# Spreading per-token scales over all partitions through DRAM instead of TensorE transposes, in an audio tower on one core

## The chip, the cores and the metric

The kernel runs on one core of a Trainium2 chip. A core has five engines with queues of their own: TensorE (PE in the profile; PEld is its loading of stationary operands), VectorE (DVE), ScalarE (ACT), GpSimd (POOL) and SyncE (SP), which issues most DMAs. They wait for one another by semaphores only. SBUF is the working memory of 128 partitions, PSUM holds what TensorE writes, and DRAM lies outside of the core. The metric is the device time of one execution in microseconds (us), a median over runs.

## What is computed

The input is 64 clips of 80000 samples. Each clip is padded and cut into 157 frames of 512 samples, which are the tokens, of width 512. One layer follows:

```
h = frames @ DCT.T                        # tokenizer, float32
n = (h - mean) / sqrt(var + 1e-5)         # layer norm over the 512 features of a token
V, g = n @ Wv + bv, sigmoid(n @ Wg + bg)
kp, qp = tanh(n @ Wk + bk) * pi, tanh(n @ Wq + bq) * pi
total = causal sums over tokens of V, weighted by cos(key phase - query phase), and by position
total = g * total + (1 - g) * positional part, divided by sqrt(8 * position)
h = h + n + total @ Wo + bo
m = layer norm of h
e = argmax of softmax(mean over tokens of m @ Wg2 + bg2)   # one of 16 experts per clip
h = h + score[e] * (m @ We[e] + be[e])
```

All of it is in float32.

## The kernel before

**Tiling.** The clips go in 16 groups of `GB` = 4. The tokens of a clip are padded to 160, five blocks of 32; a tile of 128 partitions holds one block of each of the four clips, so a group has five tiles: 0 to 3 and `TAIL` (4). The samples of a group lie in `xT` with the features on the partitions and the 640 tokens in the free dimension, in two halves of 320 (`half`).

**Where the scale comes in.** The layer norm needs 1 / deviation of every token (`rstd`). The DCT is linear and its weights are already less their mean, so the kernel projects the *samples* with the DCT folded into `wv`, `wg` and `wkq`, and multiplies the samples by 1 / deviation first. A token's deviation is found from the tokens laid on partitions (`embed`, then `statistics`: two VectorE instructions and three small ones on GpSimd, with a fourth in `embed_statistics`), so it is a column, one value per partition. The samples need it as a row, the same in all 128 partitions. `scale_all` does that turn: six TensorE transposes of a broadcast column against the identity (L298) leave the rows in PSUM, and two VectorE multiplications (L304) scale the halves of `xT`.

**Stages of a group g from the second on.** `project_and_values(g)`: phases and value products from `xT` (with `turn_x2(g-1, n)` between them, which turns the normalized block n of the group before by four transposes, L690, for its expert). `gate(g)`. `experts_and_embedding(g)`: the expert products of group g-1 (L817), one block at a time, and between them the embedding and statistics of group g+1. `attention(g)`: `read` (L614) sums the values over tokens, then come the output products. Group 0 has its own opening (`first_values`, `first_gate`).

**The output products.** `attention` multiplies by `Wo` in the Strassen-Winograd manner: seven products (`output_product`, L372) in the order 1, 2, 6, 7, 4, 5, 3. Products 3, 6 and 7 take sums of tokens that `token_sums` makes on VectorE, one or two at a `next(made)`: sums 0 and 1 (product 6), 2 (product 7), 3 (product 3). The last tile has its own product (`output_tail`, L237) after product 1. VectorE adds each product from PSUM to the residual, whose quarters are `r11`, `r12` (blocks 0 and 1) and `r21`, `r22` (blocks 2 and 3). After product 7, three additions go to GpSimd (`more`, L630; on VectorE in the last group); products 4 and 5 are added to `r21` and `r22` behind them. After product 5 `statistics2` takes blocks 2 and 3, and `normal2` normalizes a block on ScalarE (L677). `scale_all(g+1)` stands after product 7.

**What sets the order.** The order of the program is that of the Python code (`manual_schedule`): every engine takes its instructions in that order, and the framework puts in the semaphore waits between engines. Buffers rotate: `psum()` gives one of four PSUM tiles in turn, and a TensorE product waits until the tile's last reader is done. Tiles of one tag share buffers in the same way; `even` has two.

Of the kernel before, what the change touches and what calls it, by code (L numbers as in the profile page):

```python
# [14 lines left out]
F32 = mybir.dt.float32  # L15
I32 = mybir.dt.int32
AF = mybir.ActivationFunctionType
ALU = mybir.AluOpType
# [4 lines left out]
P = 128  # L23
C = D // P
H = D // 2
GB = 4
NG = B // GB
LP = 160
Q = P // GB
NM = LP // Q  # L30
TAIL = NM - 1
SLOT = [0, 1, 3, 4, 2]
HT = P // 2
HN = HT + 2 * P
# [19 lines left out]
def audio_tower(ctx: ExitStack, tc: tile.TileContext, a, out):  # L54
# [21 lines left out]
    nc = tc.nc  # L76
    ctx.enter_context(tc.manual_schedule())
    pool = lambda name, bufs, **kw: ctx.enter_context(tc.tile_pool(name=name, bufs=bufs, **kw))
    const = pool("const", 1)
    p1 = pool("p1", 1)  # L80
    p2 = pool("p2", 2)
    small = pool("small", 8)
    ps_mm = pool("ps_mm", 4, space=bass.MemoryType.PSUM)

    def load(name, shape, src=None):
        t = const.tile(shape, F32, name=name, tag=name)
# [3 lines left out]
    def psum():  # L90

        return ps_mm.tile([P, 2, 512], F32, tag="mm", name="mm")
# [4 lines left out]
    S = [{} for _ in range(NG)]  # L97
# [120 lines left out]
        sub(raw, raw, ps.unsqueeze(1).to_broadcast([P, C, n]))  # L218


    def statistics(h):

        st = small.tile([P, 6], F32, tag="st", name="st")
        nc.vector.bn_stats(st, h)
        mv = small.tile([P, 2], F32, tag="mv", name="mv")
        nc.vector.bn_aggr(mv, st)  # L226
        rstd = small.tile([P, 1], F32, tag="rstd", name="rstd")
        nc.gpsimd.tensor_scalar(rstd, mv[:, 1:2], EPS, None, ALU.add)  # L228
        nc.gpsimd.tensor_tensor(rstd, rstd, power, ALU.pow)  # L229
        shift = small.tile([P, 1], F32, tag="shift", name="shift")  # L230
        nc.gpsimd.tensor_scalar(shift, mv[:, 0:1], rstd, -1.0, ALU.mult, ALU.mult)  # L231
        return rstd, shift

    def by_tokens(ps, x, n, w):

        for c in range(C):
            nc.tensor.matmul(ps, tile_of(x[:, c], n), w[:, c, :], start=(c == 0), stop=(c == C - 1))  # L237
        return ps


    def embed(g, n):
# [15 lines left out]
    def embed_statistics(g, n):  # L257
        s = S[g]
        h, odd = s.pop(("h", n))
        by_r = h.rearrange("p (j r) -> p r j", r=4)  # L260
        sines = p2.tile([P, P + 1], F32, tag="sines", name="sines")
        nc.scalar.copy(sines, odd[:, 1, : P + 1])
        add(by_r[:, 1, :], odd[:, 0, :P], sines[:, :P])
        sub(by_r[:, 3, :], odd[:, 0, 1 : P + 1], sines[:, 1 : P + 1])
        rstd, shift = statistics(h)
        rstd1 = small.tile([P, 1], F32, tag="rstd1", name="rstd1")
        nc.gpsimd.tensor_scalar(rstd1, rstd, 1.0, None, ALU.add)  # L267
        s["rstd", n] = rstd
        s["st", n] = h, shift, rstd1

    def embed_res(g, n):

        s = S[g]
        h, shift, rstd1 = s.pop(("st", n))
        if n == TAIL:
            r = p1.tile([P, D], F32, tag="res_t", name="res_t", bufs=2)
        else:
            if n % 2 == 0:
                s["res2"].append(p1.tile([P, 2, D], F32, tag="res", name="res", bufs=6))
            r = s["res2"][-1][:, n % 2, :]  # L280
        nc.scalar.activation(r, h, AF.Identity, bias=shift, scale=rstd1)  # L281
        s["res"][n] = r

    def add_bo(g, n):
        r = S[g]["res"][n]
        nc.gpsimd.tensor_tensor(r, r, bo, ALU.add)  # L286

    def scale_all(g):

        s = S[g]  # L290
        ps = psum()
        lo = 0

        for n in (0, 1, TAIL, TAIL, 2, 3):
            rows = slice(0, P) if n != TAIL else slice(0, HT) if lo < HN - 1 else slice(HT, P)
            m, at = divmod(lo, HN)
            w = rows.stop - rows.start
            nc.tensor.transpose(  # L298
                ps[:, m, at : at + w], s["rstd", n][rows].to_broadcast([w, P]), ident[rows, rows]
            )  # L300
            lo += w
        for m in range(2):
            x = half(s["xT"], m)
            nc.vector.tensor_tensor(x, x, ps[:, m, :HN].unsqueeze(1).to_broadcast([P, C, HN]), ALU.mult)  # L304


    def quarters(w):
# [316 lines left out]
    def output_product(g, i):  # L624

        s = S[g]
        ps = product(g, i, fac_o)
        (r11, r12), (r21, r22) = ([r[:, :, n : n + H] for n in (0, H)] for r in s["res2"])
        last = g + 1 == NG
        more = lambda to, x: (nc.vector if last else nc.gpsimd).tensor_tensor(to, to, x, ALU.add)  # L630
        if i == 1:
            s["u"] = [p2.tile([P, 2, H], F32, tag="u", name="u") for _ in range(2)]
            nc.scalar.copy(s["u"][0], ps)  # L633
        first, second = s["u"]
        if i in (1, 2):
            add(r11, ps, r11)
            if last and i == 2:
                add_bias(g - 1, ORDER[0])
        elif i == 6:
            add(first, ps, first)  # L640
        elif i == 7:
            add(second, ps, first)
            more(r22, second)
            more(r21, second)
            more(r12, first)
        elif i == 5:
            add(r22, ps, r22)
            if last:
                add(r12, ps, r12)
            for n in (2, 3):  # L650
                statistics2(g, n)
            if not last:
                add(r12, ps, r12)
        elif i == 3:
            add(r12, ps, r12)
        else:
            add(r21, ps, r21)
# [150 lines left out]
    def add_bias(g, n):  # L808

        s = S[g]  # L810
        nc.vector.scalar_tensor_tensor(s["res"][n], s["be"], s["gate"], s["res"][n], ALU.mult, ALU.add)
# [25 lines left out]
    def expert(g, n, between=lambda c: None):  # L837
        ps = psum()
        for c in range(C):
            between(c)  # L840
            expert_chunk(g, n, c, ps[:, 0, :])
        between(C)
        expert_out(g, n, ps[:, 0, :])
# [82 lines left out]
    def first_gate():  # L926

        made = chain(weight_sums(wv, t_v), weight_sums(wo, t_o))

        def weights():  # L930
            next(made)
            next(made)

        gate_part(0, 0)
        weigh()
        fold_twice(1, 1)
        add_bo(0, 0)
        gate_part(0, 1)
        weights()
        scores(0)  # L940
        embed(1, 2)
        embed_statistics(1, 2)
        embed_res(1, 2)
        add_bo(0, 1)
        weights()
        weights()
        gate_part(0, 2)
        for n in (3, TAIL):
            embed(1, n)
            embed_statistics(1, n)  # L950
        for n in (3, TAIL):
            embed_res(1, n)
        weights()
        gate_part(0, 3)
        for n in (2, 3, TAIL):
            add_bo(0, n)
        load_half(2, 0)
        load_half(2, 1)
# [62 lines left out]
    def experts_and_embedding(g):  # L1021

        new = g + 1

        def embedded(n):
            embed_statistics(new, n)
            embed_res(new, n)

        add_bias(g - 1, TAIL)
        expert(g - 1, TAIL)  # L1030
        for n in range(3):
            embed(new, n)
            embed_statistics(new, n)
        add_bias(g - 1, 0)
        for n in range(3):
            embed_res(new, n)
        add_bv(g, 0)
        load_half(g + 2, 0)
        load_half(g + 2, 1)
        expert(g - 1, 0)  # L1040
        add_bias(g - 1, 1)
        add_bv(g, 1)
        expert(g - 1, 1)
        embed(new, 3)
        embed(new, TAIL)
        embed_statistics(new, 3)
        embed_statistics(new, TAIL)
        embed_res(new, 3)
        embed_res(new, TAIL)
        add_bias(g - 1, 2)  # L1050
        expert(g - 1, 2)
        add_bias(g - 1, 3)
        expert(g - 1, 3)

    def attention(g):
        ahead = g + 1 < NG
        if ahead and g > 0:
            for n in range(NM):
                add_bo(g + 1, n)
        for c in range(C):  # L1060
            read(g, c)
        S[g]["blocks"] = halves(S[g]["gT"])
        made = token_sums(g, tail=False)
        if g == 0:
            for n in range(NM):
                add_bo(1, n)
        for i in (1, 2, 6, 7, 4, 5, 3):
            output_product(g, i)
            if i == 1:
                next(made)  # L1070
                next(made)
                output_tail(g)
                statistics2(g, TAIL)
            elif i in (2, 6):
                next(made)
                if i == 6:
                    normal2(g, TAIL)
            elif i == 7 and ahead:
                scale_all(g + 1)
        for n in (0, 1):  # L1080
            statistics2(g, n)
        normal2(g, 2)
        normal2(g, 3)
# [170 lines left out]
```

## Time and profile before

The median is 1384.3 us over three runs (1384.22 to 1384.72); the profiled execution spans 1382.9 us, with the TensorE clock granted in full.

| what | from the profile |
|---|---|
| TensorE, VectorE, ScalarE, GpSimd busy | 99%, 75%, 29%, 44% of the span |
| transposes of the scale, L298 | 96, in 16 groups |
| multiplications of the samples, L304 | 32, 1.48 us each (median) |
| additions on GpSimd, L630 | 45, 1.27 us each |
| DMA from DRAM of half a group's samples, 640 KB | 4.5 us from issue to landing |
| DMA of an output block, 64 KB | 1.7 us |

A row of the groups reads: line, engine, operation, out<-in by the program's names, shapes, count, and after the bar the busy time in us, the mean ns of one, and the idle time of the engine just before with what ended it. A row of the timeline reads: start and duration in us, engine, line, operation, names, shapes, count, and in brackets the idle time before it and its releaser. Rows of one kind that follow each other are merged. Starts on TensorE are pipelined: the next matmul starts before the row's end, so the cost of a matmul in the queue is the distance between starts, not its duration.

### The profile page before, as it was taken

How to read it: one execution, taken by the hardware profiler on the slowest of the kernel's cores; microseconds unless marked ns; L12 is line 12 of the kernel's file. 1: busy time of each engine (PE TensorE's matmuls, PEld its weight loads, DVE VectorE, ACT ScalarE, POOL GpSimd, SP SyncE). 2: the span in 40 equal slices, each digit the busy share in tenths (PEclk: the TensorE clock that was granted, in tenths of full speed). 3: DMA queues.
4: the chain of work that ended last, by engine and by line, in shares of the span. 5: the costliest groups of instructions: out<-in, count | busy, mean ns of one | idle time of the engine just before them, and what ended most of it. 6: DMA issues, size and time to landing. Idle time of an engine off the chain costs nothing.

```text
span 1382.9 us, 26934 instructions
## 1 busy us (share of the span) xinstructions
PE 1374.0 (99%) x10656; PEld 918.0 (66%) x10656; DVE 1031.8 (75%) x2076; ACT 403.3 (29%) x690; POOL 607.2 (44%) x858
## 2 busy tenths in 40 slices
PE   9999999999999999999999999999999999999998
PEld 5676575866758567575765758667585675757763
DVE  5888786877868677786777868778686777867673
ACT  2514142231423214242141422314232142421410
POOL 2462554425453354544525544254533535445314
PEclk9999999999999999999999999999999999999999
DMA  6013214032230413205032140322304132040306
GB/s 224 1 39 130 76 55 145 9 135 72 108 99 1 169 38 130 77 3 188 16 130 77 52 146 9 136 72 115 91 1 157 50 130 77 4 150 16 130 9 197
DMA packets 47292, 119.70 MB, mean 87 GB/s; under 512 B 9264, under 2 KB 26304, under 8 KB 39232
## 3 DMA queue, kind: packets, MB, share of 16 engines
q0 software_dynamic: 11456, 72.10, 13.6%
q1 hardware_dynamic: 35212, 45.26, 11.1%
q8 instruction: 84, 1.38, 0.4%
q10 hardware_dynamic: 500, 0.64, 0.2%
q14 instruction: 40, 0.33, 0.1%
HBM read 97.39 MB, written 20.58 MB: 85 GB/s over the span
## 4 chain that ended last, share of the span: by engine, by line
PE 99%; DVE 0%; DMA 0%; issue 0%; SPq 0%
PE mm L372 27%; PE mm L817 21%; PE mm L579 17%; PE mm L614 9%; PE mm L237 9%; PE mm L252 3%; PE mm L690 3%; PE mm L524 3%; PE mm L254 3%; PE mm L560 1%; PE mm L598 1%; PE mm L298 1%; PE mm L198 1%; DMA wv<-in_wv 0%; PE mm L709 0%; PE mm L736 0%
## 5 line engine op out<-in xcount | busy, mean ns | idle before, releaser
L817 PE MATMUL mm<-we,x2T 128*32 128x512 f32 x2400 | 268.1, 594 | 0.4 <-issue 0.4
L228 POOL TENSOR_SCALAR rstd<-mv 128x1 f32<-128x1 f32 x160 | 42.8, 267 | 508.0 <-DVE mv L226 498.0
L817 PEld LDWEIGHTS mm<-we,x2T 128*32 128x32 f32 x2400 | 73.3, 110 | 162.6 <-issue 158.4
L99 DVE TENSOR_TENSOR gT<-mm,gT 128x128 f32<-128x128 f32 (+1 forms) x135 | 87.0, 673 | 82.3 <-PE mm L579 80.9
L622 DVE TENSOR_TENSOR gT<-mm,gT 128x320 f32<-128x320 f32 x256 | 116.9, 488 | 26.1 <-PE mm L614 21.7
L614 PE MATMUL mm<-att,v 32*128 32x256 f32 (+3 forms) x2048 | 124.1, 360 | 0.0
L614 PEld LDWEIGHTS mm<-att,v 32*128 32x128 f32 x2048 | 105.2, 185 | 22.8 <-ACT res_t L281 6.7
L589 ACT ACTIVATE gT<-gT,hbg 128x320 f32<-128x320 f32 x120 | 59.7, 556 | 168.2 <-DVE gT L99 168.2
L229 POOL TENSOR_TENSOR rstd<-rstd,power 128x1 f32<-128x1 f32 x160 | 98.3, 614 | 13.3
L828 DVE SCALAR_TENSOR_TENSOR res<-mm,gate,res 128x512 f32<-128x512 f32 x64 | 48.0, 750 | 73.1 <-PE mm L817 63.8
L677 ACT ACTIVATE x<-res,shift,rstd 128x512 f32<-128x512 f32 x64 | 52.1, 816 | 142.7 <-DVE res L99 126.1
L771 POOL DMA_INDIRECT we<-in_we,rows x60 | 62.2, 1036 | 71.3 <-DVE rows L767 57.6
L372 PE MATMUL mm<-t_o,sum 128*128 128x256 f32 x384 | 88.3, 379 | 0.4 <-DVE sum L98 0.4
L121 POOL TENSOR_TENSOR xT<-xT 128x640 f32<-128x640 f32 x30 | 46.8, 1559 | 91.6 <-DVE even L99 84.7
L99 DVE TENSOR_TENSOR v<-mm,v 128x512 f32<-128x512 f32 x105 | 70.8, 686 | 18.8 <-PE mm L372 18.4
L372 PE MATMUL mm<-t_v,sum 128*128 128x256 f32 x360 | 82.7, 379 | 0.0
L286 POOL TENSOR_TENSOR res<-res,bo 128x512 f32<-128x512 f32 x64 | 82.2, 1314 | 0.0
L231 POOL TENSOR_SCALAR shift<-mv,rstd 128x1 f32<-128x1 f32 x160 | 73.8, 461 | 16.6
L281 ACT ACTIVATE res<-mm,shift,rstd 128x512 f32<-128x512 f32 x64 | 49.8, 778 | 104.2 <-POOL rstd L267 79.7
L372 PEld LDWEIGHTS mm<-t_o,sum 128*128 128x128 f32 x384 | 71.9, 190 | 11.7 <-PE mm L372 0.8
L99 DVE TENSOR_TENSOR res<-mm,res 128x512 f32<-128x512 f32 x96 | 65.2, 685 | 15.0 <-ACT u L633 11.8
L630 POOL TENSOR_TENSOR res<-res,u 128x512 f32<-128x512 f32 x45 | 56.0, 1273 | 42.1 <-DVE u L99 42.1
(199 smaller groups left out, 2799.2 us busy)
## 6 DMA issues: line engine op xcount, KB each, us to landing
xT<-in_frames SPq DMA_DIRECT2D x32, 640.0 KB, 4.5
out<-res SPq DMA_DIRECT2D x236, 64.0 KB, 1.7
out<-res_t SPq DMA_DIRECT2D x62, 32.0 KB, 1.6
out<-res_t SPq DMA_DIRECT2D x62, 26.0 KB
wv<-in_wv SPq DMA_DIRECT2D x2, 512.0 KB, 6.0
wg<-in_wg SPq DMA_DIRECT2D x1, 1024.0 KB
wo<-in_wo SPq DMA_DIRECT2D x1, 1024.0 KB
we<-in_we,rows POOLq DMA_INDIRECT x60
```

Source lines behind the costliest of these rows:

```text
L99: add = lambda *x: nc.vector.tensor_tensor(*x, ALU.add)
L229: nc.gpsimd.tensor_tensor(rstd, rstd, power, ALU.pow)
L231: nc.gpsimd.tensor_scalar(shift, mv[:, 0:1], rstd, -1.0, ALU.mult, ALU.mult)
L237: nc.tensor.matmul(ps, tile_of(x[:, c], n), w[:, c, :], start=(c == 0), stop=(c == C - 1))
L286: nc.gpsimd.tensor_tensor(r, r, bo, ALU.add)
L372: nc.tensor.matmul(ps[:, b, :], lhs[:, c, P * b : P * (b + 1)], w[:, c, :], start=(c == 0), stop=(c == 1))
L579: nc.tensor.matmul(ps[:, o, :HN], w[:, c, o * P : (o + 1) * P], rhs[:, c], start=(c == 0), stop=(c == 1))
L589: nc.scalar.activation(to, to, AF.Tanh, bias=hbg[:, c : c + 1], scale=0.5)
L614: nc.tensor.matmul(to, s["v", n][q, c * P : (c + 1) * P], by, start=(n == 3), stop=(n == TAIL))
L622: nc.vector.tensor_tensor(th, r[:, :, n], th, op)
L771: nc.gpsimd.indirect_dma_start(out=ws[b][:, n * k : n * (k + 1)], out_offset=None, in_=of, in_offset=bass.IndirectOffsetOnAxis(ap=rows[:, ...
L817: nc.tensor.matmul(ps[Q * i : Q * (i + 1), :], s["x2T"][:, c, i, Q * n : Q * (n + 1)], s["ws"][i][:, c, :], start=(c == 0), stop=(c == C - 1),
```

## The change

From group 1 on the turn of the scale goes another way. `statistics` writes 1 / deviation of the new group straight into a column of a 128x32 tile (`deviations`, two of them in turn, set to zero at the start). `keep_deviations` transposes this tile on VectorE, in blocks of 32x32, so that each clip's values become rows of 32, and four small DMAs write them to DRAM in the order of the samples' tokens. `spread_deviations` reads that row of 640 values back into all partitions with one DMA, into an `even` buffer. The purpose is that TensorE has no transposes for it. `scale_all` then multiplies the samples by this SBUF tile. It is called after product 1, ahead of the last tile's product, with all three of the first token sums ahead of it; the fourth sum is made after product 7. In product 7 the addition to `r21` goes ahead of that to `r22`. Group 0 keeps its transposes.

```diff
+    dram = pool("dram", 2, space=bass.MemoryType.DRAM)
...
-    def statistics(h):
+    def statistics(h, rstd=None):
...
-        rstd = small.tile([P, 1], F32, tag="rstd", name="rstd")
+        if rstd is None:
+            rstd = small.tile([P, 1], F32, tag="rstd", name="rstd")
...
+    deviations = [const.tile([P, Q], F32, name=f"dev{k}", tag=f"dev{k}") for k in range(2)]
+    for x in deviations:
+        nc.gpsimd.memset(x, 0.0)
...
-        rstd, shift = statistics(h)
+        if g == 0:
+            to = None
+        else:
+            to = deviations[g % 2][:, SLOT[n] : SLOT[n] + 1]
+        rstd, shift = statistics(h, to)
...
+    def keep_deviations(g):
+
+        turned = p2.tile([P, Q], F32, tag="turned", name="turned")
+        nc.vector.transpose(turned, deviations[g % 2])
+        S[g]["row"] = row = dram.tile([NM, GB, Q], F32, tag="row", name="row")
+        for i in range(GB):
+            nc.sync.dma_start(out=row[:, i], in_=turned[Q * i : Q * i + NM])
+
+    def spread_deviations(g):
+
+        s = S[g]
+        s["scale"] = scale = p2.tile([P, 2, HN], F32, tag="even", name="scale")
+        row = s.pop("row").rearrange("s b t -> (s b t)")
+        nc.sync.dma_start(out=scale.rearrange("p m t -> p (m t)"), in_=row.partition_broadcast(P))
...
         for m in range(2):
             x = half(s["xT"], m)
-            nc.vector.tensor_tensor(x, x, ps[:, m, :HN].unsqueeze(1).to_broadcast([P, C, HN]), ALU.mult)
+            nc.vector.tensor_tensor(x, x, scale[:, m, :HN].unsqueeze(1).to_broadcast([P, C, HN]), ALU.mult)
...
             add(second, ps, first)
+            more(r21, second)
             more(r22, second)
-            more(r21, second)
             more(r12, first)
...
+        keep_deviations(1)
+        spread_deviations(1)
         weights()
         gate_part(0, 3)
...
         expert(g - 1, 2)
+        keep_deviations(new)
         add_bias(g - 1, 3)
         expert(g - 1, 3)
+        spread_deviations(new)
...
             if i == 1:
-                next(made)
-                next(made)
+                for _ in range(3):
+                    next(made)
+                if ahead:
+                    scale_all(g + 1)
                 output_tail(g)
                 statistics2(g, TAIL)
-            elif i in (2, 6):
+            elif i == 6:
+                normal2(g, TAIL)
+            elif i == 7:
                 next(made)
-                if i == 6:
-                    normal2(g, TAIL)
-            elif i == 7 and ahead:
-                scale_all(g + 1)
```

More of the change, by code (lines that the diff above doesn't have):

```diff
@@ L286, in add_bo @@
         nc.gpsimd.tensor_tensor(r, r, bo, ALU.add)
+    def keep_deviations(g):
[9 more added lines that the diff above has]
+        nc.sync.dma_start(out=scale.rearrange("p m t -> p (m t)"), in_=row.partition_broadcast(P))
     def scale_all(g):
         s = S[g]
[L291 to L301, printed above, removed]
+        if g == 0:
+            scale = psum()
+            lo = 0
+            for n in (0, 1, TAIL, TAIL, 2, 3):
+                rows = slice(0, P) if n != TAIL else slice(0, HT) if lo < HN - 1 else slice(HT, P)
+                m, at = divmod(lo, HN)
+                w = rows.stop - rows.start
+                nc.tensor.transpose(
+                    scale[:, m, at : at + w], s["rstd", n][rows].to_broadcast([w, P]), ident[rows, rows]
+                )
+                lo += w
+        else:
+            scale = s.pop("scale")
         for m in range(2):
             x = half(s["xT"], m)
-            nc.vector.tensor_tensor(x, x, ps[:, m, :HN].unsqueeze(1).to_broadcast([P, C, HN]), ALU.mult)
+            nc.vector.tensor_tensor(x, x, scale[:, m, :HN].unsqueeze(1).to_broadcast([P, C, HN]), ALU.mult)
     def quarters(w):
```

## The prediction

> **What bounds the kernel now.** I read the page's busy shares first, then the chain of waits, then TensorE's groups with shapes kept apart, and last the timeline of one middle group, since what the change is worth is decided there.
>
> ```profile
> PE 1374.0 (99%) x10656; PEld 918.0 (66%) x10656; DVE 1031.8 (75%) x2076; ACT 403.3 (29%) x690; POOL 607.2 (44%) x858
> ...
> PE 99%; DVE 0%; DMA 0%; issue 0%; SPq 0%
> ```
>
> TensorE is busy 99% of the span and is 99% of the chain that ended last: a matmul taken away shortens the run by its place in TensorE's queue, as long as no other engine then makes TensorE wait. The groups of TensorE give the work that is removed:
>
> ```profile
> L298 PE MATMUL mm<-ident,rstd 128*128 128x128 f32 x64 | 13.0, 285 | 0.0
> L298 PE MATMUL mm<-ident,rstd 64*128 64x64 f32 x32 | 4.3, 266 | 0.0
> ```
>
> That is 96 transposes, 6 in each of 16 groups of clips. Their durations overlap, so their cost is read from the starts around them. The timeline of the output products of a middle group, columns start, duration, engine, line, operation:
>
> ```profile
> 512.04 0.94 PE L298 MATMUL mm<-ident,rstd 128*128 128x128 f32 x6
> ...
> 512.24 0.69 DVE L99 TENSOR_TENSOR u<-mm,u 128x512 f32<-128x512 f32 x1 [0.44 <-PE mm L372]
> ...
> 512.82 1.03 PE L372 MATMUL mm<-t_o,gT 128*128 128x256 f32 x4
> ...
> 513.02 3.73 POOL L630 TENSOR_TENSOR res<-res,u 128x512 f32<-128x512 f32 x3 [2.81 <-DVE u L99]
> 513.02 2.89 DVE L304 TENSOR_TENSOR xT<-xT,mm 128x1280 f32<-128x1280 f32 x2
> ...
> 515.83 1.35 DVE L99 TENSOR_TENSOR res<-mm,res 128x512 f32<-128x512 f32 x2
> ...
> 517.21 0.69 DVE L224 BATCH_NORM_STATS2 st<-res 128x6 f32<-128x512 f32 x1
> ...
> 519.49 0.81 ACT L677 ACTIVATE x<-res,shift,rstd 128x512 f32<-128x512 f32 x1 [8.42 <-DVE res L99]
> ...
> 520.84 0.42 PEld L690 LDWEIGHTS mm<-ident,x 128*128 128x128 f32 x4 [0.49 <-ACT x L677]
> ```
>
> The six transposes start at 512.04 and product 4 at 512.82, so they hold TensorE's queue for 0.78 us. The later lines are a chain off TensorE that must end before TensorE turns the normalized block 2: the last sum into `r22` on VectorE, its statistics, the power on GpSimd, the normalization on ScalarE. ScalarE ends at 520.30 and TensorE starts on it at 520.84, so the chain has 0.54 us to spare. Line L690 names ScalarE as the releaser, but it had been done for half a microsecond: the gap there is TensorE's own change from 64 columns to 128.
>
> **What the skill says.** The Trainium skill, "TensorE: Matmul & The Clock Gate", Part 4: PE-mode transpose, gives about 275 ns for a transpose inside a kernel; the trace agrees on the duration (285 and 266 ns), but in the queue six take 780 ns, 130 each. "VectorE: DVE Perf Modes", the section on SBUF-source latency, gives fp32 `tensor_tensor` as (N+151)/0.96 ns and no slower mode for either memory: 1.49 us for 1280 elements, against 2.89 for two here with PSUM as second input. "SBUF — State Buffer", § two separate sides: VectorE with two SBUF inputs and a GpSimd operation that reads SBUF lock each other out; who starts first keeps the ports. This trace agrees:
>
> ```profile
> 491.15 0.74 DVE L811 SCALAR_TENSOR_TENSOR res<-be,gate,res 128x512 f32<-128x512 f32 x1
> ```
>
> ```profile
> 491.30 1.74 POOL L286 TENSOR_TENSOR res<-res,bo 128x512 f32<-128x512 f32 x1
> ```
>
> GpSimd's addition overlaps that VectorE instruction by 0.59 us and takes 1.74 instead of its median 1.27, 0.47 more. "DMA: Bandwidth & Descriptors", § Anatomy of one DMA, prices a DMA at 2.0 us plus bytes at 436 GB/s (stated for GpSimd's queue); the page here has 1.7 us for 64 KB and 4.5 us for 640 KB, the same order.
>
> **Removed.** 15 groups times six transposes (group 0 keeps its own): 15 x 0.78 = 11.7 us of TensorE, all on the path. The two multiplications of the samples only move, and read SBUF in place of PSUM, at the same price by the formula.
>
> **Added, and hidden.** A transposition of 128x32 on VectorE after the output of expert block 2: no row of the trace shows one; the skill's VectorE page, § The three transpose paths, has 311 ns for a 128x128 bf16, so an estimate of 0.1 to 0.35 us; I take 0.2. It stands where VectorE is idle 2.02 us before its next output at 493.91. It waits for GpSimd's last power of the new group, done at 490.22 + 0.57 = 490.79, before the engine gets there at 491.2. Five DMAs on SyncE: four small rows take about 0.44 us each to issue (1.73 us for four output DMAs), so from 492.9 to 494.7, landing near 497 at 2 us. The spread of 320 KB waits for them and lands between 2.75 us (estimate by the skill's price) and 4.5 us (the 640 KB row) later, by 502. VectorE first needs it near 506.8. Nothing urgent is queued behind it on SyncE: the next output is one group of experts away. Two memsets at the start lie beside the loads. So all of this costs nothing.
>
> **Moved: VectorE's order.** Between product 1 and product 4 VectorE now does: sum of product 1, token sums 0, 1, 2, both multiplications, the last tile's sum and statistics, product 2, 6, 7, token sum 3. I lay the durations of the timeline one behind the other (a start 0.61 after a 512-wide start, 0.72 where it needs the one before, 1.41 for each multiplication), from 504.25: token sums at 504.86, 505.57, 506.18; multiplications at 506.8 and 508.2; last tile at 509.6 (507.06 before); product 2 at 511.3, product 6 at 511.9, product 7 at 512.7, ending 513.36 where it ended 512.93. Token sum 3 follows to 513.96.
> TensorE isn't held by this directly: the last tile's PSUM is free at 510.3, product 4 wants it at 511.8; product 3 wants token sum 3 at 515.3.
> But GpSimd's three additions `res<-res,u` wait for product 7, and start at 513.45 instead of 513.02, under token sum 3, which reads SBUF twice. By the L286 case they lose about 0.38 us (0.51 of overlap less the same 0.13). The edit to `more` puts `r21` first, which lets VectorE's sum for product 4 go at about 515.1, and makes `r22` second of the three: done at 513.45 + 0.38 + 1.22 (start to start) + 1.27 = 516.32, and VectorE's sum into it starts at 516.36. It started at 516.49 before (second of the pair that ends 517.18, less 0.69). The chain to block 2 thus moves 0.13 us earlier, and ends at 520.17, plus 0.12 us from a semaphore to TensorE (in the last group a token sum ended 1327.83 and the load began at 1327.95): 520.29. TensorE would be there at 520.84 - 0.78 = 520.06. It waits 0.23 us. Bounds: nothing, if the lock or my spacings are 0.25 us less; 0.6 us if the multiplications cost 0.1 more each and GpSimd loses the whole 0.51. Later waits, of blocks 3, 0 and 1, keep 0.3 us or more.
>
> **Last group.** There product 7 waited for token sum 2 (TensorE started at 1327.98 instead of 1327.41); the earlier sum saves that 0.57, and token sum 3, now behind three additions on VectorE, gives about 0.27 back: 0.3 saved.
>
> **The sum.** 11.7 - 15 x 0.23 + 0.3 = 8.5 us: 1384.3 - 8.5 = 1375.8.
>
> **Rivals.** (a) No wait at all: 11.7 + 0.3 saved, 1372.3. For it: 0.54 us to spare before, and 0.23 is within what laying durations end to end can miss. Against: GpSimd's second addition isn't earlier than 515.9 even without the lock.
> (b) The chain is later than I have it and TensorE waits 0.6 us: 15 x 0.18 + 0.3 = 3.0, 1381.3; or VectorE, 13.51 us busy between 501.49 and 517.80, 16.31 us of TensorE time, becomes the bound and nothing is gained, 1384. For it: the stage is VectorE's densest. Against: it needs every unknown at its worse end.
> (c) Slower: the round trip through DRAM lands after VectorE asks for it, and all PSUM evacuations queue behind that wait. From the issue at 497 there are 9.8 us; 11 us would put VectorE 1.2 late, TensorE 1.2 + 0.23 - 0.78 = 0.65 later per group, 15 x 0.65 = 9.8: 1394. Against: no DMA of this size in steady groups takes half as long, and the DMA share between 501 and 518 is zero.
>
> **How the numbers follow.** The forecast 0.47, (a) 0.30, (b) 0.17, (c) 0.06. The range runs from (a), 1372.0, to 1380.0, most of (b). Faster by over 0.2% (under 1381.5): the forecast, (a) and two thirds of (b), 0.88; within: 0.06; slower: 0.06.
>
> **What would show it.** Right: no L298 outside the first group; TensorE's product 4 one step after product 7; a first load of L690 on block 2 waiting some 0.2 us for ScalarE; the group's period (the transposes of two groups start at 428.07 and 512.02, 83.94 apart) at 83.4 us; additions L630 with one of 1.6 us in each group. Wrong: `r22` summed later than 516.5 in the same place, a DMA named as releaser of the multiplications, or L304 much over 1.49 us.

## The result, and the profile after

| | before | after |
|---|---|---|
| median time, us | 1384.26 (1384.01 to 1384.72, 4 runs) | 1372.42 (1371.99 to 1372.54, 4 runs) |
| ratio after / before | | 0.9914, 95% interval 0.9896 to 0.9931 |
| span of the profiled execution, us | 1382.9 | 1370.6 |

The change saves 11.8 us. That is inside the range of the prediction (1372.0 to 1380.0), but 3.4 us under its forecast of 1375.8, and 0.1 us from what rival (a), "no wait at all", gave. The lines of the code have moved: in the changed kernel L333 is a multiplication of the samples, L302 the transposition on VectorE, L305 and L312 the DMAs to and from DRAM, L659 an addition on GpSimd, L706 the normalization, L719 the turn of a normalized block, L401 an output or value product, L553 the projection of the phases, L99 and L100 additions on VectorE.

The page of the changed kernel, its busy times and the engines' shares of the chain that ended last:

```profile
PE 1362.6 (99%) x10566; PEld 912.5 (67%) x10566; DVE 1040.9 (76%) x2091; ACT 402.8 (29%) x690; POOL 604.3 (44%) x860
...
PE 96%; DVE 2%; ACT 1%; POOL 1%; issue 0%; DVEq 0%; POOLq 0%
...
scale<-row SPq DMA_DIRECT2D x15, 320.0 KB
```

TensorE's 90 instructions are gone and its busy time is 11.4 us shorter. It is still the bound. Of the chain that ended last 4% now runs through other engines, where before had 1%, but not in the steady groups: 31 us of it lie in the first 115 us (11 in before), 17 us in the one group, near 675 us, that is shown below, and the rest at the end. Everywhere else the chain is TensorE alone, as before. The groups, with shapes kept apart, show what is left of the transposes, all of it in the first group:

```profile
L325 PE MATMUL mm<-ident,rstd 128*128 128x128 f32 x4 | 0.8, 285 | 0.0
L325 PE MATMUL mm<-ident,rstd 64*128 64x64 f32 x2 | 0.3, 266 | 0.0
```

Where the time went is read from the starts of the same TensorE instruction in both traces. The period of a group is 83.162 us instead of 83.946: 0.784 less in each of 15 groups, 11.76 in all. The rest is small: start-up 0.45 earlier (loads that the change doesn't touch arrived earlier), 0.27 lost in the first group, 0.32 lost in one later group, 0.46 won in the last group, and 0.2 in the closing DMAs. These add up to the 12.3 us between the spans.

The same middle group as in the prediction, in the timeline of the changed kernel. The starts are 4.11 us earlier than those of before for equal work:

```profile
487.05 0.20 DVE L302 STREAM_TRANSPOSE turned<-dev 128x32 f32<-128x32 f32 x1
...
487.16 5.42 POOL L297 TENSOR_TENSOR res<-res,bo 128x512 f32<-128x512 f32 x4
487.18 1.82 DVE L840 SCALAR_TENSOR_TENSOR res<-be,gate,res 128x512 f32<-128x512 f32 x1
...
488.98 1.28 SPq L305 DMA_DIRECT2D row<-turned  x4
...
492.56 0.35 SPq L312 DMA_DIRECT2D scale<-row  x1
...
502.68 2.89 DVE L333 TENSOR_TENSOR xT<-xT,scale 128x1280 f32<-128x1280 f32 x2
...
505.48 0.68 DVE L100 TENSOR_TENSOR res_t<-mm,res_t 128x512 f32<-128x512 f32 x1
...
506.93 0.18 DVE L227 BATCH_NORM_AGGREGATE mv<-st 128x2 f32<-128x6 f32 x1
507.03 0.66 DVE L100 TENSOR_TENSOR res<-mm,res 128x512 f32<-128x512 f32 x1
...
507.60 1.47 DVE L100 TENSOR_TENSOR u<-mm,u 128x512 f32<-128x512 f32 x2
...
508.99 0.68 DVE L99 TENSOR_TENSOR sum<-gT,sum 128x512 f32<-128x512 f32 x1
509.16 4.10 POOL L659 TENSOR_TENSOR res<-res,u 128x512 f32<-128x512 f32 x3 [0.74 <-DVE u L100]
...
512.06 0.69 DVE L100 TENSOR_TENSOR res<-mm,res 128x512 f32<-128x512 f32 x1 [0.54 <-POOL res L659]
...
515.06 0.81 ACT L706 ACTIVATE x<-res,shift,rstd 128x512 f32<-128x512 f32 x1 [5.79 <-POOL shift L233]
...
515.95 0.42 PEld L719 LDWEIGHTS mm<-ident,x 128*128 128x128 f32 x4 [0.49 <-ACT x L706]
515.96 0.66 PE L719 MATMUL mm<-ident,x 128*128 128x128 f32 x4
```

The scale makes its round trip between 487.05 and 502.68 with no wait: L333 has no releaser, and the last packet of the 320 KB is in at 495.56, 7.1 us before VectorE wants it. The lines at the end decide the gain. ScalarE finishes block 2 at 515.87 (515.06 + 0.81), TensorE begins to load it at 515.95. Between them lie 0.08 us, where before had 0.54. A semaphore takes about 0.05 of that (the distance in the experiments where TensorE is seen to wait), so some 0.03 us is to spare. The load has the same 0.49 in its bracket as in before, where ScalarE had long been done; the matmuls of L719 have no bracket: TensorE didn't wait. In one of the 15 groups it did:

```profile
675.06 0.69 DVE L100 TENSOR_TENSOR u<-mm,u 128x512 f32<-128x512 f32 x1 [0.46 <-DVE u L100]
...
681.73 0.81 ACT L706 ACTIVATE x<-res,shift,rstd 128x512 f32<-128x512 f32 x1 [6.14 <-DVE res L100]
...
682.60 0.66 PE L719 MATMUL mm<-ident,x 128*128 128x128 f32 x4 [0.26 <-ACT x L706]
```

There VectorE's sum of product 7 began 0.35 us late, everything behind it moved by as much, and TensorE lost 0.32. That is 0.35 less 0.03, a second sign of how little was to spare.

### The profile page after: what moved, and what is told of

It is laid out like the page before. It is cut to its first block, busy times and chain, and to the rows that moved or that the text cites. A ratio compares the mean times of both kernels' runs of the same rounds, so it can differ in the third digit from the quotient of the medians.

```text
span 1370.6 us, 26797 instructions
## 1 busy us (share of the span) xinstructions
PE 1362.6 (99%) x10566; PEld 912.5 (67%) x10566; DVE 1040.9 (76%) x2091; ACT 402.8 (29%) x690; POOL 604.3 (44%) x860
## 4 chain that ended last, share of the span: by engine, by line
PE 96%; DVE 2%; ACT 1%; POOL 1%; issue 0%; DVEq 0%; POOLq 0%
PE mm L401 27%; PE mm L846 21%; PE mm L608 17%; PE mm L643 9%; PE mm L239 9%; PE mm L259 3%; PE mm L719 3%; PE mm L553 3%; PE mm L261 2%; PE mm L627 1%; PE mm L199 1%; PE mm L188 0%; PE mm L738 0%; PE mm L765 0%; PE mm L212 0%
## 5 line engine op out<-in xcount | busy, mean ns | idle before, releaser
L100 DVE TENSOR_TENSOR gT<-mm,gT 128x128 f32<-128x128 f32 (+1 forms) x135 | 86.9, 672 | 81.9 <-PE mm L608 80.4
L230 POOL TENSOR_SCALAR dev<-mv 128x1 f32<-128x1 f32 x75 | 25.4, 339 | 260.8 <-DVE mv L227 255.5
L230 POOL TENSOR_SCALAR rstd<-mv 128x1 f32<-128x1 f32 x85 | 20.6, 242 | 268.7 <-DVE mv L227 265.8
L100 DVE TENSOR_TENSOR res<-mm,res 128x512 f32<-128x512 f32 x96 | 65.1, 680 | 38.8 <-POOL res L659 25.4
L800 POOL DMA_INDIRECT we<-in_we,rows x60 | 58.9, 982 | 77.0 <-issue 58.6
L401 PE MATMUL mm<-t_o,sum 128*128 128x256 f32 x384 | 88.1, 379 | 0.0
L297 POOL TENSOR_TENSOR res<-res,bo 128x512 f32<-128x512 f32 x64 | 85.3, 1362 | 0.0
L100 DVE TENSOR_TENSOR v<-mm,v 128x512 f32<-128x512 f32 x105 | 70.5, 683 | 18.3 <-PE mm L401 18.3
L401 PE MATMUL mm<-t_v,sum 128*128 128x256 f32 x360 | 82.7, 379 | 0.0
L706 ACT ACTIVATE x<-res,shift,rstd 128x512 f32<-128x512 f32 x64 | 52.1, 815 | 103.6 <-DVE res L100 75.6
L401 PEld LDWEIGHTS mm<-t_o,sum 128*128 128x128 f32 x384 | 73.0, 190 | 9.9
L239 PE MATMUL mm<-wv,xT 128*128 128x512 f32 x160 | 72.1, 593 | 0.0
L401 PEld LDWEIGHTS mm<-t_v,sum 128*128 128x128 f32 x360 | 66.1, 190 | 7.7
```

The source lines that it names most:

```text
L100: add = lambda *x: nc.vector.tensor_tensor(*x, ALU.add)
L401: nc.tensor.matmul(ps[:, b, :], lhs[:, c, P * b : P * (b + 1)], w[:, c, :], start=(c == 0), stop=(c == 1))
L706: nc.scalar.activation(x, s["res"][n], AF.Identity, bias=shift, scale=rstd)
L800: nc.gpsimd.indirect_dma_start(out=ws[b][:, n * k : n * (k + 1)], out_offset=None, in_=of, in_offset=bass.IndirectOffsetOnAxis(ap=rows[:, ...
```

## Experiments

The theory after the result: the transposes cost their distance in TensorE's queue and nothing else was gained, and the new order is what keeps the chain to block 2 from taking the gain back. The rivals: the new order itself gains; the multiplications gain by reading SBUF; the hidden additions are not free, only covered by something. The first four kernels ran beside a kernel before at 1384.21 us, the three after them at 1385.06, the last at 1385.11. The changed kernel is set against them by its ratio and by its period.

**The order without the new route.** Before, with the order of the changed kernel; the transposes stay.

```diff
+            more(r21, second)
             more(r22, second)
-            more(r21, second)
...
             if i == 1:
-                next(made)
-                next(made)
+                for _ in range(3):
+                    next(made)
+                if ahead:
+                    scale_all(g + 1)
                 output_tail(g)
                 statistics2(g, TAIL)
-            elif i in (2, 6):
+            elif i == 6:
+                normal2(g, TAIL)
+            elif i == 7:
                 next(made)
-                if i == 6:
-                    normal2(g, TAIL)
-            elif i == 7 and ahead:
-                scale_all(g + 1)
```

> The kernel before with only the new order: multiplications after product 1, token sums around them, r21 first on GpSimd; the six transposes of a group stay, now behind product 1. If the saving is the transposes' place in TensorE's queue (0.78 us in each of 15 groups), nearly nothing is gained: only the last group's wait for token sum 2, 0.46 us, so 1383.8 us. If the order itself saved the time, most of 11.8 us would show: under 1376.

Measured: 1383.96 us, ratio 0.9999 (0.9991 to 1.0008), period 83.95. The order alone gains nothing that can be measured. GpSimd's first addition takes 1.64 us here too, so the lock by the fourth token sum comes with the order, not with the new route.

**The new route without the order.** The changed kernel with the old order of `attention` and of `more`: the lines of the diff above, reversed.

> The changed kernel with the old order: the multiplications stand after product 7, at the moment of GpSimd's three additions, and read SBUF twice. If VectorE with two SBUF inputs keeps GpSimd off SBUF, the additions start after both multiplications, some 2.6 us late; r21 and r22 follow, block 2 is ready 2.3 us later than in the kernel before, TensorE waits about 2.5 us in each of 15 groups and gives back far more than the 0.78 it saves: about 1408 us. If the order was put in for no reason that shows, the time is that of the changed kernel, 1372.4.

Measured: 1408.41 us, ratio 1.0176 (1.0159 to 1.0193), period 85.55. Without its order the route through DRAM is 24 us slower than before. The group of the multiplications, and the timeline of the same group of clips:

```profile
L333 DVE TENSOR_TENSOR xT<-xT,scale x30: 1481/2018/2564, 93.1 to 1292.5; 128x1280 f32<-128x1280 f32 x30
```

```profile
521.21 3.96 DVE L333 TENSOR_TENSOR xT<-xT,scale 128x1280 f32<-128x1280 f32 x2
521.38 6.15 POOL L659 TENSOR_TENSOR res<-res,u 128x512 f32<-128x512 f32 x3 [2.81 <-DVE u L100]
...
526.33 1.29 DVE L100 TENSOR_TENSOR res<-mm,res 128x512 f32<-128x512 f32 x2 [1.17 <-POOL res L659]
...
529.93 0.81 ACT L706 ACTIVATE x<-res,shift,rstd 128x512 f32<-128x512 f32 x1 [10.51 <-DVE res L100]
530.80 0.66 PE L719 MATMUL mm<-ident,x 128*128 128x128 f32 x4 [1.35 <-ACT x L706]
```

The numbers of the first line are least, median and greatest, in ns. The multiplications, now with two inputs in SBUF, stand beside GpSimd's additions, and the two engines take turns. The first multiplication holds until 522.69 (521.21 + 1.48). GpSimd's first addition, started at 521.38, ends at 523.82, 2.44 long. The second multiplication waits for that and ends at 525.17 (521.21 + 3.96), 2.56 long. The second addition waits for that in its turn: 2.52. Only the third takes 1.27. In before the same two rows stand side by side and keep their lengths (3.73 and 2.89, in the prediction), since there the multiplications have one input in PSUM. The wait shows as a longer duration, not as idle time with a releaser: engines don't wait for one another by semaphores only. The Trainium skill, "SBUF — State Buffer", § two separate sides, says that of a VectorE operation with two SBUF inputs and a GpSimd operation that reads SBUF, the one that starts first has the ports for its whole instruction and the other blocks; this run agrees, and shows that it goes in turns, both ways. The sum into block 2 then comes late, and TensorE waits 1.35 us here, and 0.90 us for VectorE at the projection (L553) ahead of it. The time is the expected one (about 1408), but the path is only in part: the additions don't start after both multiplications, they take turns with them, and TensorE waits at two places. So the number was right partly by luck. This kernel undoes the whole order at once; what the place of the multiplications costs with the rest of the new order kept was not run.

**Six transposes put back.** The changed kernel, with six transposes of the same shapes behind product 7. Nobody reads what they write, so they take time on TensorE and, as in before, one PSUM tile, and nothing else.

```diff
             elif i == 7:
                 next(made)
+                if ahead:
+                    idle = psum()
+                    for k in range(6):
...
+                        nc.tensor.transpose(
+                            idle[:, k // 3, P * (k % 3) : P * (k % 3) + n],
+                            deviations[0][rows, 0:1].to_broadcast([n, P]),
+                            ident[rows, rows],
+                        )
```

> The changed kernel with six transposes of unused values put back behind product 7, their result read by nobody. If the saving is their place in TensorE's queue and nothing else, the period of a group returns from 83.16 to 83.95 us and the time to 1372.4 + 15 x 0.78 = 1384.1 (less 0.3 for the one group that waited). If part of the saving was in the multiplications' or the evacuations' waits, it stays clearly under 1383.

Measured: 1383.79 us, ratio 0.9998 (0.9989 to 1.0007), period 83.95. The whole gain is gone again, 0.79 us per group for six transposes. So the transposes' place in the queue is all of it; a multiplication that reads SBUF instead of PSUM gains nothing (1.483 us against 1.481 in before).

**The old order of two additions.** The changed kernel with `r22` ahead of `r21`.

```diff
+            more(r22, second)
             more(r21, second)
-            more(r22, second)
             more(r12, first)
```

> The changed kernel with GpSimd's additions in the old order, r22 before r21. VectorE takes r21 first, so it now waits for the second addition there and comes to r22 0.61 us later (one addition's place on VectorE). If the chain from r22 to the normalized block 2 has only some 0.03 us to spare, TensorE waits 0.58 us per group: 1372.4 + 8.7 = 1381.1, and the load of block 2's first transpose starts within 0.1 us of ScalarE's end in every group. If it still has 0.5 us to spare, as in the kernel before, there is no difference: 1372.4 to 1373.5.

Measured: 1380.84 us, ratio 0.9976 (0.9967 to 0.9986), period 83.74. Two lines in the other order cost 8.4 us, 71% of the gain. In the timeline of the same group:

```profile
512.77 4.10 POOL L659 TENSOR_TENSOR res<-res,u 128x512 f32<-128x512 f32 x3 [0.74 <-DVE u L100]
...
519.27 0.81 ACT L706 ACTIVATE x<-res,shift,rstd 128x512 f32<-128x512 f32 x1 [6.39 <-DVE res L100]
520.13 0.66 PE L719 MATMUL mm<-ident,x 128*128 128x128 f32 x4 [0.51 <-ACT x L706]
```

GpSimd works as long as in the changed kernel (4.10), but VectorE's sum of product 4 now waits for GpSimd's second addition, and its sum into block 2 goes after that one. TensorE waits in every group, and its step to L719 is 0.94 us where the changed kernel has 0.36: 15 x 0.58 = 8.7, less the 0.32 of the group that waits in any case, is 8.4. This wait is as long as the prediction's upper bound (0.6), and the order in `more` is enough to bring it about. TensorE starts 0.05 us after ScalarE's end (519.27 + 0.81 = 520.08): the semaphore.

**The fourth token sum earlier.** The changed kernel with token sum 3 between products 6 and 7, out of GpSimd's way.

```diff
             elif i == 6:
+                next(made)
                 normal2(g, TAIL)
-            elif i == 7:
-                next(made)
```

> The changed kernel with token sum 3 between the sums of product 6 and product 7, so that it no longer runs as GpSimd's additions begin. If the long first addition (1.64 us against 1.27) comes from that sum's two SBUF reads, all three additions take 1.27; they start 0.4 us later, so r22 moves by no more than 0.1 us and the time stays at 1372 to 1373. If the first addition is long for another reason (the start after an idle stretch), it stays at 1.64 and TensorE waits 0.4 us more per group: 1378.

Measured: 1373.19 us beside 1385.06, ratio 0.9913 (0.99 to 0.9927), period 83.18. The additions' group:

```profile
L659 POOL TENSOR_TENSOR res<-res,u x45: 1259/1269/1284, 93.6 to 1260.9; 128x512 f32<-128x512 f32 x45
```

No addition is over 1.284 us now, where the changed kernel has one of 1.64 in each group. That shows the cause of the 1.64, but it doesn't show in the time: the token sum stands ahead of product 7's sum on VectorE instead, and GpSimd starts later by about what it then saves (0.4 us).

**Two and four copies more on the way.** The changed kernel, with the row of 640 values copied on from DRAM to DRAM two or four times before it is spread (`range(4)` in the second kernel).

```diff
-        row = s.pop("row").rearrange("s b t -> (s b t)")
+        row = s.pop("row")
+        for _ in range(2):
+            further = dram.tile([NM, GB, Q], F32, tag="further", name="further")
+            nc.sync.dma_start(out=further, in_=row)
+            row = further
+        row = row.rearrange("s b t -> (s b t)")
```

> The changed kernel with the row copied twice more from DRAM to DRAM, each copy waiting for the one before, ahead of the spread. In the changed kernel the spread's last packet ends 7.1 us before VectorE needs it. At an estimated 2.3 us for a copy and its wait, two copies leave 2 us: no change, 1372.4. If the round trip is already near the edge, the multiplications wait for a DMA and the time goes over 1380.

> The same with four copies: 4 x 2.3 = 9.2 us against 6.6 us to spare (7.1 less the time in which the landing is told), so VectorE waits about 2.6 us for the spread in each group, all behind it moves, and TensorE waits as long: 1372.4 + 15 x 2.6 = 1411. If the transfer is not needed until later than VectorE's place suggests, or if the copies are shorter (under 1.6 us), there is no change.

Measured: two copies 1373.17 us, ratio 0.9916 (0.9901 to 0.9931), period 83.16 and no wait for a DMA; four copies 1395.19 us, ratio 1.0071 (1.0056 to 1.0086). The second was expected at 1411: the direction is right, the size is not. In its timeline:

```profile
500.45 4.74 SPq L314 DMA_DIRECT2D further<-further  x3
506.53 0.35 SPq L317 DMA_DIRECT2D scale<-further  x1
...
510.03 2.89 DVE L338 TENSOR_TENSOR xT<-xT,scale 128x1280 f32<-128x1280 f32 x2 [1.52 <-DMA scale<-further]
```

A copy that waits for the one before takes 2.03 us from issue to issue (a third of 506.53 - 500.45), not the 2.3 I had reckoned, which is about what the changed kernel has from the end of the rows' issue to that of the spread (490.26 to 492.56). So four of them delay by 8.1 us, and VectorE waits 1.5 us here instead of 2.6. Over 14 groups it waits 21.2 us, between 0.8 and 3.3 in each; the first group hardly waits. The distance to the kernel with two copies is 22.0. This shows what lies behind rival (c): about 7 us to spare, nothing lost within them, and beyond them VectorE's wait comes through in full. Most of it, 17.7 us, reaches TensorE as a wait at the turn of block 2, whose chain stands behind VectorE's wait.

**Block 2 turned later.** The kernel with `r22` first, and the turn of block 2 put one value product later, to take the wait away from the other side.

```diff
         project(g)
-        turn_x2(g - 1, 2)
...
         value_product(g, 1)
+        turn_x2(g - 1, 2)
         turn_x2(g - 1, 3)
```

> The changed kernel with r22 first on GpSimd, as in the run that cost 8.4 us, but with block 2 turned after value product 1 instead of before it: TensorE has 1.73 us of other work while ScalarE ends the block. If all of the 8.4 us was TensorE's wait for block 2, it vanishes: 1372 to 1373. If it was something that a later place doesn't hide (a PSUM tile not yet free, or VectorE behind for the rest of the group), most of it stays: 1378 or more.

Measured: 1376.78 us, ratio 0.994 (0.9926 to 0.9954), period 83.40: of the 0.58 us that a group had lost, 0.34 are won back, where I had expected nearly all. The expectation failed because a wait took the place of the one removed:

```profile
517.52 1.59 PEld L401 LDWEIGHTS mm<-wv,xT 128*128 128x128 f32 x8 [0.49 <-issue]
...
519.27 0.56 ACT L720 COPY x2T<-mm 128x512 f32<-128x512 f32 x1
...
519.88 0.42 PEld L719 LDWEIGHTS mm<-ident,x 128*128 128x128 f32 x4 [0.17 <-ACT x2T L720]
```

TensorE no longer waits for block 2, but ScalarE is still late: it normalizes blocks 2 and 3 before it copies the last tile's turn out of PSUM (L720), and that PSUM tile is the one in which TensorE would turn block 3. It is what the expectation had named as the other case, a PSUM tile not yet free. That costs some 0.15 of the 0.24 us per group that are left. The rest, some 0.09, lies in two steps on TensorE that became longer without a named wait; why was not settled.

The first line also bears out a reading in the prediction. The load behind the phases' projection has 0.49 us of idle time here too, and here it is a value product's, which waits for nothing ("issue"). So the 0.49 at block 2 in before was not a wait for ScalarE. At both places the matmuls change from 64 columns to 128, as the prediction says; no run takes that change apart from the rest.

No kernel of these is faster than the changed one by more than can be measured.

## Why the prediction was nearly right

**Removed: right.** 0.78 us per group was forecast and 0.784 measured, and putting six transposes back took it away again.

**Added and hidden: right, but at a higher price than stated.** The transposition takes 0.20 us, as taken. It also moves the expert sum behind it (L840, 487.18) to just after the start of GpSimd's addition (487.16), so that this time VectorE is held up: the sum takes 1.82 us where in before, in this group, it took 0.74 and GpSimd lost instead. A sum of over 1.8 us stands in 13 groups, and before has none. The prediction put that at nothing; it stays hidden because VectorE still has 0.89 us of idle time before its next output, instead of 2.02. The four rows took 1.28 us to issue rather than 1.73, the 320 KB were in 3.0 us after their issue, inside the bounds of 2.75 and 4.5. No multiplication waits for a DMA, and 7.1 us were to spare where the prediction had about 4.8 (506.8 less 502).

**Moved: right in every step but one, and that one set the forecast.** The prediction's starts of VectorE's queue, less 4.11, beside the measured ones:

| step | forecast | measured |
|---|---|---|
| last tile's sum | 505.49 | 505.48 |
| sum of product 2 | 507.19 | 507.03 |
| first sum of products 6 and 7 | 507.79 | 507.60 |
| GpSimd's additions | 509.34 | 509.16 |
| second addition done | 512.21 | 512.03 |
| sum into `r22` | 512.25 | 512.06 |
| ScalarE done with block 2 | 516.06 | 515.87 |
| TensorE takes block 2, without a wait | 515.95 | 515.96 |

Up to the last tile the queue is right to 0.01 us over seven instructions; then a step is too long, and 0.19 too much is carried to the end. The term is the distance from the last tile's aggregate to the sum of product 2. I took 0.27 us for it from the trace of before (508.52 to 508.79). But there VectorE was waiting for product 2, which TensorE had only just ended; it was a wait, not the price of the step. The trace of before has the step without a wait too, in the same group, as 0.10 (an aggregate at 518.73, a sum at 518.83). Once the same instructions were bunched behind the multiplications, product 2 had long been done, and the step took 0.10 us (506.93 to 507.03). The other mis-sized term is the semaphore to TensorE, 0.12 in the sum and 0.05 measured. With both, the wait of 0.23 us per group isn't there: 15 x 0.23 = 3.45, and the forecast was 3.4 too high. The prediction named this as the lower bound ("nothing, if the lock or my spacings are 0.25 us less"), and it was the spacings, with the semaphore for the last 0.07. With 0.03 us left, it was close that the whole gain came through. The lock was sized right: the first addition takes 1.64 us, 0.37 longer than 1.27, for a forecast of 0.38.

**Last group: right in kind, small in size.** 0.46 instead of 0.3: TensorE no longer waits for token sum 2, as forecast, and the fourth sum gives back less.

**Not foreseen: the first group.** There the transposition stands on VectorE in front of other work at a time when GpSimd is not yet done with group 1's deviations:

```profile
72.45 0.21 DVE L302 STREAM_TRANSPOSE turned<-dev 128x32 f32<-128x32 f32 x1 [0.99 <-POOL dev L231]
...
74.78 2.09 PE L643 MATMUL mm<-att,v 32*128 32x320 f32 x26 [0.28 <-ACT res_t L292]
```

VectorE waits 0.99 us, what is queued behind it runs into GpSimd's small operations, and TensorE waits 0.28 us for ScalarE at the end. The prediction had looked at a middle group and the last. In size it is a fortieth of the gain.

Of the prediction's five signs of being right, three came: no L298 outside the first group, product 4 one step (1.73 us) after product 7, and one addition of 1.6 us in each group. The two that hang on the wait did not: TensorE doesn't wait 0.2 us for block 2, and the period is 83.16 us, not 83.4.

**The rivals.** (a) is what happened, for the reason given for it (what laying durations end to end can miss). (b) and (c) didn't come about, but are near: `r22` first gives a wait of 0.58 per group, (b)'s size, though for a reason that (b) didn't name; a longer way through DRAM gives +10 us over before, by (c)'s own path. The new route with the whole old order gives +24, by a path that no rival had: the two engines' turns at SBUF. What stays open is why VectorE's sum of product 7 was 0.35 us late in one group of 15. It is not the place in the program: the kernels with token sum 3 earlier and with two copies more have no such group in their traces.

## What to carry to other kernels

Work taken off the engine that bounds the kernel is worth its distance between starts, and it comes through in full only if the chains beside it still end in time: here by 0.03 us, so lay out the chain that will then be level with the bound before promising the gain. An operand that moves from PSUM to SBUF costs nothing by itself, but can bring VectorE and GpSimd into each other's way, so it has to be moved in time as well. When you take a spacing out of a trace to lay out a queue that doesn't exist yet, ask of each gap whether the engine needed it or was waiting; a gap that was a wait must not be carried over.

## What the runs showed of the hardware

- The turns that VectorE and GpSimd take at SBUF go both ways, by whole instructions: an addition of 1.27 us becomes 2.44 and 2.52, a multiplication of 1.48 becomes 2.56, and in the changed kernel an expert sum of 0.74 becomes 1.82. I had expected only GpSimd to lose.
- Small copies from DRAM to DRAM (2.5 KB), each waiting for the one before, follow each other at 2.03 us; 320 KB spread over all partitions from a row in DRAM are there 3.0 us after the issue.
- From ScalarE's end to the start of a TensorE load that waits for it, 0.05 us (520.08 to 520.13, with `r22` first).
- On VectorE, an instruction that doesn't need the one before can start ahead of that one's end (the sum at 507.03 starts 0.08 us before the aggregate ends at 507.11).
